# Heads of 64: one projection for both parts of the rotary embedding, exchange of rows by DMA

## The chip, the cores and the metric

The kernel runs on 1 core of one Trainium2 chip. The metric is device time in microseconds (us) of one execution: median 3802.96 us of three runs of the kernel before (3797.84 to 3808.43). All 12 stages of a network of four layers are one program.

## What is computed

Twelve residual stages on a sequence of 2048 tokens with 128 channels: for each of four layers a half-weighted feed-forward part, an attention part, and the feed-forward part again. The change touches only the attention of the last layer (16 heads of 64, causal, keys and values from a latent of 64):

```python
q = jnp.einsum('bsd,qd->bsq', x, wq).reshape(B, S, H, D).transpose(0, 2, 1, 3)
kv_latent = jnp.einsum('bsd,ld->bsl', x, w_kv_down)
k = jnp.einsum('bsl,ql->bsq', kv_latent, w_k_up).reshape(B, S, H, D).transpose(0, 2, 1, 3)
v = jnp.einsum('bsl,ql->bsq', kv_latent, w_v_up).reshape(B, S, H, D).transpose(0, 2, 1, 3)
q = q * cos + _rotate_half(q) * sin
k = k * cos + _rotate_half(k) * sin
scores = jnp.einsum('bhsd,bhtd->bhst', q, k) / jnp.sqrt(jnp.float32(D))
scores = scores + causal[None, None]
probs = jax.nn.softmax(scores.astype(jnp.float32), axis=-1).astype(q.dtype)
out = jnp.einsum('bhst,bhtd->bhsd', probs, v)
```

Here `_rotate_half(x)` is `concatenate([-x[32:], x[:32]])` over the 64 entries of a head: each head's two halves of 32 are exchanged, one with its sign turned.

## The kernel before

The 2048 tokens lie in four chunks of 512 columns (`NC = 4`, `CH = 512`), each with its channels or head entries on the 128 partitions. In `attn3` two heads of 64 fill the 128 partitions: a head pair `p` (8 of them) and a chunk `c` of queries make one iteration, `its = [(p, c)]`, 32 in all. Each iteration needs the rotated q and k of its pair and chunk, each as a rounded part and the rest of the rounding (`h` in fp32r, and what the rounding left out), because the scores are made of three products of such parts.

**The projections.** `make(m)` returns four pieces for iteration `m`: for q and for k, half 0 and half 1. Each half is a projection into its own PSUM bank: half 0 with the weights, half 1 with weights whose rows are exchanged within each head on the host (`swapped`), so that half 1 delivers the rotated partner entries. q takes three matmuls (`product`, L227 to L229), k two (`latents`, L1744 and L1745). VectorE multiplies each bank by its table, cosine for half 0 and signed sine for half 1 (L1782). `whole` (L1792) adds the two on GpSimd. `high` rounds on ScalarE (L1797), takes the rest on GpSimd (L1798), and SP stores both to DRAM (L1799, L1800). `load` (L1858) brings them back in the layout that the scores use. The tables are 2 x 256 KB an iteration, fetched anew (L1687) after the last multiply of k. Buffers: `rot0` two, `rot1` and both tables one. Weights of a pair are fetched and split into a rounded part (VectorE, L218) and a rest (GpSimd, L222) once per pair.

**The planner.** `flash` writes the whole stage out in one order: a first pass that makes scores and their row maxima (L1069 on TensorE, L1087 on VectorE), and a second pass that makes the scores anew (L1171), takes exponentials (L1179 on ScalarE), sums them on VectorE or GpSimd (L1984) and multiplies by the values (L1136). Its TensorE instructions keep the order of the program. PSUM has two double banks for the first pass and three banks (`s2`) that the second pass, the projections (`rot`) and the small products share.

Between these steps `fill` inserts pieces. It has a clock of its own, which counts matmul columns. A piece may come when `SPACE` has passed since the last one, and while fewer are made than progress plus `AHEAD` iterations asks for. Work that has to wait for another engine is put into `timed`, with a due time `LATER` after it was entered; a new piece first runs all but the last entry of `timed`. So the pieces come densely at first, until the lead of 12 iterations is reached, and then at the pace of the iterations. The pieces of the first three iterations are made while the feed-forward stage before still runs (`for c in range(NC - 1)`). A scheduler then orders each engine's queue; each queue runs in order, and all DMAs here are issued from SP's.

Of the kernel before, what the change touches and what calls it, by code (L numbers as in the profile page):

```python
# [17 lines left out]
P = 128  # L18
# [3 lines left out]
NC = 4  # L22
# [42 lines left out]
def tile_macaron(ctx: ExitStack, tc: tile.TileContext, a: dict, out: bass.AP, stages=STAGES):  # L65
# [1632 lines left out]
    def pre_attn3(k, pool):  # L1698
        wdn = split(fetch(pool, "l3d", 0, P), pool, "wdn")
        return wdn, fetch(pool, "l3q", 0, 4 * P, "raw", 1)  # L1700

    def attn3(io, k, w, early):
# [3 lines left out]
        SPACE, AHEAD, LATER, SHARE = 1300.0, 12, 9000.0, 2  # L1706
# [30 lines left out]
        def weights(p):  # L1737
            if p not in pw:
                raw = fetch(early, "l3q", p * 4 * P, (p + 1) * 4 * P, "raw", 1)
                pw[p] = split(raw, early, "pw", 1)  # L1740
# [6 lines left out]
        def scratch(dt, name):  # L1747
            return early.tile([P, CH], dt, name=name, tag=name, bufs=2 if name == "rot0" else 1)
# [13 lines left out]
        def make(m):  # L1762
            p, c = its[m]
            halves = {}

            def half(what, i):
                while i == 0 and len(timed) > 1:
                    timed.pop(0)[1]()
                if what == "q" and i == 0:
                    halves["tabs"] = tabs_of.pop()  # L1770
                    if c == 0:
                        weights(p)
                wh, wl = pw[p]
                o = (2 * (what == "k") + i) * P
                w = tuple(t[:, o : o + P] for t in (wh, wl))
# [5 lines left out]
                t = scratch(F32R, f"rot{i}")  # L1781
                nc.vector.tensor_tensor(t.bitcast(F32), ps, halves["tabs"][i], ALU.mult)  # L1782
                halves[i] = t
                if i == 1:
                    if what == "k":
                        tabs_of.append(tables(scratch, "l3rope", (c + 1) % NC))
                    whole(what)

            def whole(what):
                t = halves[0]  # L1790
                f = t.bitcast(F32)
                nc.gpsimd.tensor_tensor(f, f, halves[1].bitcast(F32), ALU.add)  # L1792
                timed.append((now[0] + LATER, lambda: high(what, t)))

            def high(what, t):
                h = early.tile([P, CH], F32R, name="h", tag="t", bufs=2)
                nc.scalar.copy(h, t.bitcast(F32))  # L1797
                nc.gpsimd.tensor_tensor(t, t.bitcast(F32), h.bitcast(F32), ALU.subtract)  # L1798
                nc.sync.dma_start(out=hl[what][m][: 2 * D, :], in_=h.bitcast(F32))  # L1799
                nc.sync.dma_start(out=hl[what][m][2 * D :, :], in_=t.bitcast(F32))  # L1800
# [3 lines left out]
            return [lambda what=what, i=i: half(what, i) for what in "qk" for i in range(2)]  # L1804
# [6 lines left out]
        for c in range(NC - 1):  # L1811
# [4 lines left out]
            for _ in range(4):  # L1816
                pieces.pop(0)()
                yield 4.0
                if timed:
                    timed.pop(0)[1]()  # L1820
                    yield 1.0
# [463 lines left out]
```

## Time and profile before

| | |
|---|---|
| median of the runs | 3802.96 us |
| the profiled execution's own time | 3781.83 us |
| its span | 3779.9 us |
| mean granted TensorE clock | 0.934 |
| multiplies by the tables, L1782 (VectorE) | 128, 87.7 us, 685 ns each |
| additions, L1792 (GpSimd) | 64, 1282 ns in the median |
| rounding, L1797 (ScalarE) | 64, 619 ns in the median |
| rests, L1798 (GpSimd) | 64, 1279 ns in the median |
| first and last multiply | 2524.8 us, 3316.8 us |
| tables fetched | 66 DMAs of 256 KB |

The profile is one execution, recorded by the hardware. A group's row gives the line, engine, operation, what is written from what, the count, then busy us and mean ns of one, then the idle time of the engine just before these instructions and what ended it. PE is TensorE, PEld its weight loads, DVE VectorE, ACT ScalarE, POOL GpSimd, SPq the queue of SyncE that issues DMAs. A wait for several semaphores is put down to the one that came last by the profile; where the engine named had long been done, it was another, often a DMA. Durations of matmuls overlap, so their starts are the better measure of what one costs.

### The profile page before, as it was taken

What the parts mean: (1) busy time and instruction counts of PE and PEld (TensorE: products, weight loads), DVE (VectorE), ACT (ScalarE), POOL (GpSimd) and SP (SyncE); (2) the same over time, 40 slices, a digit from 0 to 9 for tenths busy, and PEclk for the clock granted to TensorE, in tenths of its full rate; (3) what the DMA queues carried; (4) which work ended last, traced back from release to release, by engine and by line L of the source; (5) the groups of instructions that cost most, each with busy time, mean ns of one, the idle gap of its engine ahead of it and who ended that gap; (6) DMA issues with size and microseconds to landing.
All of it is one profiled execution on the core that took longest, in us unless ns stands there. A gap on an engine that the chain in (4) does not pass through costs nothing. (4 is left out here: it accounts for less than half of the span.)

```text
span 3779.9 us, 64635 instructions
## 1 busy us (share of the span) xinstructions
PE 3450.8 (91%) x25325; PEld 1847.3 (49%) x25325; DVE 2873.0 (76%) x4793; ACT 2035.4 (54%) x3838; POOL 827.9 (22%) x830
## 2 busy tenths in 40 slices
PE   7689988979999999996999999988899999999999
PEld 5543356853333333883333333376444444444458
DVE  6578556767999997668799999654677877788862
ACT  3246722315888888332688888732333444444442
POOL 1511124010000000111000000142555445533341
PEclk9779989976999999996799999898899999999999
DMA  3410023010000000102000000012443333221010
GB/s 104 94 48 19 27 69 92 1 26 5 14 10 14 8 3 1 35 7 64 9 14 6 16 5 4 12 49 75 137 147 111 99 108 97 89 63 52 24 34 12
DMA packets 124689, 170.18 MB, mean 45 GB/s; under 512 B 25120, under 2 KB 52514, under 8 KB 124384
## 3 DMA queue, kind: packets, MB, share of 16 engines
q1 hardware_dynamic: 121824, 160.80, 14.0%
q0 software_dynamic: 2560, 5.25, 0.9%
q8 instruction: 199, 3.26, 0.4%
q14 instruction: 106, 0.87, 0.1%
HBM read 101.25 MB, written 45.87 MB: 39 GB/s over the span
## 5 line engine op out<-in xcount | busy, mean ns | idle before, releaser
L1087 DVE TENSOR_REDUCE mp<-s 128x2 f32<-128x1024 f32 (+3 forms) x1440 | 1628.1, 1181 | 115.3 <-PE s L1069 84.8
L1199 ACT ACTIVATE pt<-s 128x512 f32<-128x512 f32 (+1 forms) x2368 | 1220.4, 602 | 250.5 <-PE s L1190 155.5
L1190 PE MATMUL s<-q,km 32*128 32x512 f32 (+2 forms) x2368 | 751.9, 504 | 24.2 <-ACT pt L1199 14.2
L1136 PE MATMUL pv<-pt,v 128*32 128x256 f32 (+1 forms) x8568 | 752.6, 424 | 22.9 <-ACT ov L1568 11.3
L1069 PE MATMUL s<-km,qt 32*128 32x512 f32 (+3 forms) x2368 | 634.0, 519 | 57.5 <-DVE mp L1087 36.1
L1190 PEld LDWEIGHTS s<-q,km 32*128 32x128 f32 (+1 forms) x2368 | 329.7, 188 | 549.3 <-issue 360.6
L1179 ACT ACTIVATE pt<-s 128x512 f32<-128x512 f32 (+3 forms) x640 | 306.1, 530 | 357.0 <-PE s L1171 213.8
L143 POOL TENSOR_TENSOR rs<-rs,minus_half 128x4 f32<-128x4 f32 x56 | 57.7, 1030 | 1555.9 <-DVE rs L142 1555.0
L1136 PEld LDWEIGHTS pv<-pt,v 128*32 128x32 f32 x8568 | 171.1, 109 | 325.0 <-issue 151.8
L1984 DVE TENSOR_TENSOR sum<-sum,pt 128x512 f32<-128x512 f32 (+3 forms) x328 | 259.3, 806 | 89.0 <-ACT pt L1179 87.7
L1171 PE MATMUL s<-q,k 64*128 64x512 f32 (+3 forms) x1920 | 299.9, 403 | 16.3 <-ACT pt L1179 10.8
L1136 PE MATMUL pv<-pt,latv 128*64 128x512 f32 (+3 forms) x1280 | 310.7, 565 | 1.3 <-ACT pt L1179 1.3
L1984 POOL TENSOR_TENSOR sum<-sum,pt 128x512 f32<-128x512 f32 (+1 forms) x200 | 264.8, 1324 | 182.7 <-ACT pt L1179 179.6
L1069 PEld LDWEIGHTS s<-km,qt 32*128 32x128 f32 (+1 forms) x2368 | 241.0, 195 | 119.4 <-DVE mp L1087 79.2
L1171 PEld LDWEIGHTS s<-q,k 64*128 64x128 f32 x1920 | 161.7, 188 | 226.7 <-issue 138.3
L715 ACT ACTIVATE sg<-pg 128x1024 f32<-128x1024 f32 x72 | 73.9, 1026 | 174.3 <-PE pg L229 155.3
L1069 PE MATMUL s<-k,q 64*128 64x512 f32 (+3 forms) x640 | 132.4, 428 | 19.4 <-DVE mp L1087 19.0
L1782 DVE TENSOR_TENSOR rot<-rot,tab 128x512 f32<-128x512 f32 x128 | 87.7, 685 | 74.0 <-PE rot L229 39.4
L725 PEld LDWEIGHTS pd<-l1d,h 128*128 128x128 f32 x1152 | 139.3, 192 | 5.6
L725 PE MATMUL pd<-l1d,h 128*128 128x128 f32 x1152 | 140.1, 275 | 0.0
L717 DVE TENSOR_TENSOR h<-pu,sg 128x1024 f32<-128x1024 f32 x72 | 87.9, 1220 | 60.5 <-PE pu L229 55.5
L1171 PE MATMUL s<-q,two 64*128 64x512 f32 (+3 forms) x640 | 128.3, 369 | 0.0
(575 smaller groups left out, 4682.1 us busy)
## 6 DMA issues: line engine op xcount, KB each, us to landing
tab<-in_l3rope SPq DMA_DIRECT2D x66, 256.0 KB
q<-q SPq DMA_DIRECT2D x32, 512.0 KB
k<-k SPq DMA_DIRECT2D x32, 512.0 KB
l0e<-in_l0e SPq DMA_DIRECT2D x32, 256.0 KB
q<-h SPq DMA_DIRECT2D x32, 256.0 KB
q<-rot SPq DMA_DIRECT2D x32, 256.0 KB
k<-h SPq DMA_DIRECT2D x32, 256.0 KB
k<-rot SPq DMA_DIRECT2D x32, 256.0 KB
```

What stands on the lines that cost most here:

```text
L715: nc.scalar.activation(sg, pg, AF.Silu)
L717: nc.vector.tensor_tensor(h.rearrange("p m n -> p (m n)"), pu, sg, ALU.mult)
L725: nc.tensor.matmul(pd[:, i, :], h[:, m, i * P : (i + 1) * P], wd[:, m, :], start=m == 0, stop=m == 1,)
L1069: pe(nc.tensor.matmul(ps[:, o : o + w], lhsT, rhs[:, :w], start=True, stop=not masked))
L1087: ins = nc.vector.tensor_reduce(mp[:, r, j0 : j0 + 2, kc], both[:, :, :w], AX.X, ALU.max,)
L1136: i = pe(nc.tensor.matmul(pv[out_rows, lo:hi], lhsT, pts[j][:, lo:hi], start=kt == 0, stop=kt == nt - 1 and hi == CH))
L1171: pe(nc.tensor.matmul(outs[j][:, c0:], lhsT, rhs[:, c0:], start=i == 0, stop=i == len(terms[0]) - 1 and not diag,))
L1179: ex = nc.scalar.activation(pts[j][:, c0:], outs[j][:, c0:], AF.Exp, scale=scale)
L1190: pe(nc.tensor.matmul(ps[:, c0:], lhsT, rhs[:, c0:], start=i == 0, stop=i == len(terms) - 1 and (tiled or not diag),))
L1199: ex = nc.scalar.activation(pt[:, c0:], ps[:, c0:], AF.Exp, scale=scale)
L1782: nc.vector.tensor_tensor(t.bitcast(F32), ps, halves["tabs"][i], ALU.mult)
L1984: eng.tensor_tensor(t[:, c0:], other[:, c0:], pts[j][:, c0:], ALU.add)
```

## The change

There is one projection for q and one for k, so two pieces instead of four an iteration. Its bank is multiplied by both tables: by the sine table into `u` (`rot1`) and by the cosine table into `t` (`rot0`). The rows of `u` are exchanged within each head by four DMAs of 32 rows each, SBUF to SBUF, into `v` (`rot2`, two buffers). `whole`, which now runs from `timed`, adds `v` on GpSimd, rounds on GpSimd (a `tensor_scalar`) and takes the rest there. Since the sine is now multiplied before the rows are exchanged, its table is rolled by 32 rows on the host. The exchanged weights are gone, so a pair's weights are half as wide (256 columns instead of 512). The planner's constants change with it.

```diff
-        return wdn, fetch(pool, "l3q", 0, 4 * P, "raw", 1)
+        return wdn, fetch(pool, "l3q", 0, 2 * P, "raw", 1)
...
-        SPACE, AHEAD, LATER, SHARE = 1300.0, 12, 9000.0, 2
+        SPACE, AHEAD, LATER, SHARE = 2600.0, 12, 6000.0, 2
...
-            return early.tile([P, CH], dt, name=name, tag=name, bufs=2 if name == "rot0" else 1)
+            return early.tile([P, CH], dt, name=name, tag=name, bufs=1 if name in ("tab0", "tab1", "rot1") else 2)
...
-            def half(what, i):
-                while i == 0 and len(timed) > 1:
+            def piece(what):
+                while len(timed) > 1:
                     timed.pop(0)[1]()
...
-                t = scratch(F32R, f"rot{i}")
-                nc.vector.tensor_tensor(t.bitcast(F32), ps, halves["tabs"][i], ALU.mult)
-                halves[i] = t
-                if i == 1:
-                    if what == "k":
-                        tabs_of.append(tables(scratch, "l3rope", (c + 1) % NC))
-                    whole(what)
+                t, u = scratch(F32R, "rot0"), scratch(F32, "rot1")
+                nc.vector.tensor_tensor(u, ps, kept["tabs"][1], ALU.mult)
+                nc.vector.tensor_tensor(t.bitcast(F32), ps, kept["tabs"][0], ALU.mult)
+                v = scratch(F32, "rot2")
+                q = D // 2
+                for i in range(4):
+                    o = q * (i ^ 1)
+                    nc.sync.dma_start(out=v[q * i : q * i + q, :], in_=u[o : o + q, :])
+                if what == "k":
+                    tabs_of.append(tables(scratch, "l3rope", (c + 1) % NC))
+                timed.append((now[0] + LATER, lambda: whole(what, t, v)))
...
-                nc.gpsimd.tensor_tensor(f, f, halves[1].bitcast(F32), ALU.add)
-                timed.append((now[0] + LATER, lambda: high(what, t)))
-
-            def high(what, t):
+                nc.gpsimd.tensor_tensor(f, f, v, ALU.add)
                 h = early.tile([P, CH], F32R, name="h", tag="t", bufs=2)
-                nc.scalar.copy(h, t.bitcast(F32))
-                nc.gpsimd.tensor_tensor(t, t.bitcast(F32), h.bitcast(F32), ALU.subtract)
+                nc.gpsimd.tensor_scalar(h, f, 1.0, 0.0, ALU.mult, ALU.add)
+                nc.gpsimd.tensor_tensor(t, f, h.bitcast(F32), ALU.subtract)
                 nc.sync.dma_start(out=hl[what][m][: 2 * D, :], in_=h.bitcast(F32))
-                nc.sync.dma_start(out=hl[what][m][2 * D :, :], in_=t.bitcast(F32))
+                nc.sync.dma_start(out=hl[what][m][2 * D :, :], in_=f)
...
-            for _ in range(4):
+            for _ in range(2):
                 pieces.pop(0)()
-                yield 4.0
+                yield 5.0
                 if timed:
                     timed.pop(0)[1]()
-                    yield 1.0
+                    yield 2.0
...
-                    always or n_pieces - len(pieces) < n_pieces * progress + 4 * AHEAD
+                    always or n_pieces - len(pieces) < n_pieces * progress + 2 * AHEAD
...
-        [pairs(wq), pairs(swapped(wq)), twice(pairs(wk)), twice(pairs(swapped(wk)))], 2
+        [pairs(wq), twice(pairs(wk))], 2
```

In the changed kernel the multiplies stand on L1782 (sine) and L1783 (cosine), the exchange on L1788, the addition on L1795, the rounding on L1797, the rest on L1798 and the stores on L1799 and L1800.

## The prediction

> **What bounds the kernel now.** I read the engines' totals first, then the table of 50 us windows over the changed stage, then the timeline of TensorE there, then the groups by shape, the waits and the chain.
>
> ```profile
> PE 3450.8 (91%) x25325; PEld 1847.3 (49%) x25325; DVE 2873.0 (76%) x4793; ACT 2035.4 (54%) x3838; POOL 827.9 (22%) x830
> ```
>
> PE leads, but that is an average over twelve stages. The edited lines (L1782 and its neighbours) run from 2524.8 to 3316.8 us: a little inside the feed-forward stage before, the rest in attn3, which ends near 3630 us. There, by windows (columns: stretch, length, then busy us and instruction count of PE, PEld, DVE, ACT, POOL; granted clock; DMA share; GB/s):
>
> ```profile
> 2700.00:2750.00 50.00, 45.02 (x251) 21.59 (x250) 38.38 (x51) 16.13 (x32) 30.23 (x22) 0.90 0.40 129
> 3050.00:3100.00 50.00, 47.88 (x336) 23.70 (x332) 37.74 (x52) 22.44 (x46) 24.57 (x19) 1.00 0.39 123
> 3500.00:3550.00 50.00, 49.50 (x374) 24.53 (x370) 39.84 (x51) 24.57 (x51) 17.04 (x14) 1.00 0.12 33
> ```
>
> Three kinds of stretch are to be seen: projections packed densely (2650 to 2870), projections spread out (to 3317), none (after). Summing the windows, PE is busy 607.3 of 650 us in 2650 to 3300 (93.4%) and 194.2 of 200 us in 3350 to 3550 (97.1%). DVE stands near 78% throughout. So PE sets the pace, DVE is second, and projections bring 0.037 x 650 = 24 us of extra PE idleness besides their own matmuls.
>
> What a projection takes of PE (start, us, line, last column the count):
>
> ```profile
> 2965.97 0.50 PE L227 MATMUL rot<-xH,pwH 128*128 128x512 f32 x1
> 2966.31 0.40 PE L228 MATMUL rot<-xL,pwH 128*128 128x512 f32 x1
> 2966.54 0.39 PE L229 MATMUL rot<-xH,pwL 128*128 128x512 f32 x1
> 2966.86 0.73 PE L1069 MATMUL s<-k,q 64*128 64x512 f32 x4
> ...
> 2978.71 0.50 PE L1744 MATMUL rot<-lat,pwH 128*128 128x512 f32 x1
> 2979.05 0.40 PE L1745 MATMUL rot<-lat,pwL 128*128 128x512 f32 x1
> 2979.38 0.44 PE L1069 MATMUL s<-k,q 64*128 64x384 f32 x2
> ```
>
> Start to next start, a q half takes 0.89 us and a k half 0.67 us. Durations overlap, so their sum would overstate it.
>
> **The change, part by part.**
>
> *PE.* 64 q and 64 k projections become 32 and 32; the changed program's order has exactly 160 matmuls fewer (3 per q, 2 per k). 32 x 0.89 + 32 x 0.67 = 49.9 us, on the engine that sets the end. I book all of it, the 6 pairs in the stage before too (PE is busy 46.7 of 50 us in 2500 to 2550): **-50 us**. The planner's constants keep the rate per iteration: pieces halve, SPACE doubles, and AHEAD stays at 12 iterations.
>
> *DVE.* The multiplies stay 128 of 0.69 us; two now follow each other on one PSUM bank. The weight casts halve (8 of about 0.41, half gone): **-2 us**. The score banks of the second pass share their three buffers with the projection. PE waited for the multiply (rows "PE ... <- DVE rot L1782") 5.8+2.8+1.2+0.9+0.8+0.6 = 12.1 us in 128 halves. A bank is now held 0.69 us longer, 64 times. Bounds: -6 (half as many waits) to 64 x 0.69 = +44 (every hold reaches PE). About a quarter of the L1782 instances wait for PE or make it wait; with a third of the holds showing, 64 x 0.30 = 19 against 12: **+7 us**.
>
> *The exchange by DMA.* 4 DMAs a piece, 256 in all, each 64 KB between SBUF rows; the trace has none such. SP issues one in 0.33 us (row of L1799), so 4 take 1.3 us. Landing lies between 1.56 us (4 KB) and 3.17 us (128 KB), by the chain:
>
> ```profile
> 3432.07 1.56 DMA inv<-sum
> 3433.64 3.01 DMA rc<-inv
> 3436.91 3.18 DMA inv<-rc
> 3440.62 3.17 DMA sum<-inv
> ```
>
> I take 2.5. Two waits come from it. `rot1` has one buffer: the next piece's first multiply waits 1.3 + 2.5 = 3.8 us after the last. `rot0` has two: 1.4 (multiplies) + 3.8 + POOL 1.28 + 0.69 + 1.28 + store 0.3 + 2.5 = 11.3 us must fit two pieces. Spread out, pieces come some 16 us apart and both are hidden by flash work. In the dense stretch 68 halves took 225 us, 6.6 us a pair, and without the removed half (0.78 on average) about 5.8 us a piece: two pieces are 11.6 us, hardly any slack left. The tables wait there too: one buffer each, now both reloaded after the pair of multiplies and behind four more issues (1.4 + 1.3 + 0.7 + 2.5 to 3.2 = 5.9 to 6.6 us against 5.8), where before table 0 was freed half a piece earlier. Such stalls exist already:
>
> ```profile
> 2679.06 0.69 DVE L1782 TENSOR_TENSOR rot<-rot,tab 128x512 f32<-128x512 f32 x1 [2.23 <-PE pv L1136]
> ```
>
> PE had delivered that bank by 2676.4, so a DMA ended this wait. Behind the waiting multiply stand the row maxima (L1087), for which PE waits before it may write the next first-pass bank. In the changed program's order some 25 pieces stand densely; I take 1 us of DVE each, half of it reaching PE: **+12 us**. Bounds 0 and 25 x 3.2 = +80. SP carries 21 instead of 13 DMAs an iteration, and in the program's order each waits for the eighth before it; I leave that in the bound.
>
> *ACT.* 64 casts of 0.62 us go, with the time that ACT's queue stood behind POOL:
>
> ```profile
> ACT h L1797 <- POOL rot L1792: 152.6, 61, 6.7
> ACT pt L1179 <- PE s L1171: 202.7, 145, 5.6
> PE s L1171 <- ACT pt L1179: 10.8, 15, 2.0
> ```
>
> The 152.6 us look large, but the second row says that ACT mostly has nothing to do; PE waits for its exponentials only 10.8 us. Half of that: **-5 us** (bounds -11 and 0).
>
> *POOL.* The cast costs 64 x 0.69 = 44 us, by the row of the same operation and shape; weight remainders give back 8 x 0.65 = 5. If the cast cost as much as a two-input operation (1.28), it would be 82.
>
> ```profile
> L872 POOL TENSOR_SCALAR h<-f 128x512 fp32r<-128x512 f32 x32 | 22.0, 692 | 36.9 <-ACT f L908 27.0 <-DVE f L886 9.7
> L1984 DVE TENSOR_TENSOR sum<-sum,pt 128x512 f32<-128x512 f32 x157 | 172.7, 1100 | 53.6 <-ACT pt L1179 53.4
> ```
>
> POOL is busy about half of the stage, so 39 us more fit; what they hold up are its partial sums, hence the buffers of the exponentials (ACT waited 8.9 us for those). A DVE sum of this shape takes 0.68 us undisturbed in the timeline and 1.10 in the mean, so beside POOL it loses 0.42 x 157 = 66 us over some 540 us of POOL work; 39 more cost 66 x 39/540 = 5 us of DVE, half on the path, and 2 us for the sums: **+4 us** (bounds 0 and +20).
>
> The Trainium skill ("SBUF — State Buffer", Who interferes with whom) speaks against this part: DVE with two SBUF inputs and GpSimd share one read port as an exclusive lock, and the loser is blocked fully. The trace agrees that the sums suffer and that the multiply with a PSUM input does not (653 to 694 ns throughout). Read strictly, an added cast blocks a waiting DVE sum for its whole 0.69 us, up to 44 us; the sum would then be -34 + 20 = -14 us. I go by the row.
>
> **Sum**: -50 - 2 + 7 + 12 - 5 + 4 = -34 us. The profiled execution took 3781.83 us (span 3779.9, 1.9 around it), so 3748; the runs' median 3802.96 is 0.56% above it, and 3748 x 1.0056 = **3769 us**. All bounds together: -50 - 2 - 6 + 0 - 11 + 0 = -69 (3734) to -50 - 2 + 44 + 80 + 0 + 20 = +92 (3895).
>
> **The rivals.**
>
> *DVE stands for the DMAs (slower).* Place: the first multiply of a piece, for `rot1` or a table, behind an SP queue that itself waits (L1858 up to 17.7 us, L2005 up to 20.5 us in SP's waits). If this lasts into the spread-out stretch, all 58 attn3 pieces pay. With half reaching PE the other terms (-46) are used up at 46/29 = 1.6 us a piece; at 3 us it gives -46 + 87 = +41, or 3844 us. For: single buffers, eight more issues an iteration. Against: 16 us between spread-out pieces. Long waits would also slow PE: the granted clock was 0.68 in 2700 to 2710, where PE had gaps of 0.85 to 0.97 us, 3.2 us lost in 10.
>
> The Trainium skill ("TensorE: Matmul & The Clock Gate", The HAM clock gate) says that one idle window of about 3.4 us halves the clock; here much shorter gaps already went with a lower one, so the row is the harsher.
>
> *DVE takes over as the bound (less gain).* At 78% it has 220 us spare in 1000, but maxima and multiplies come in bursts. If only half of the PE time is won: -25 + 16 = -9, or 3794 us. For: PE already waits for L1087 (19 us). Against: DVE's load is unchanged.
>
> *The waits go as well (more gain).* Half as many pieces, half of the 24 us idleness, ACT freed: -50 - 2 - 12 - 5 + 2 = -67, or 3736 us. That the change doesn't remove the work is excluded by the count of matmuls.
>
> **How the numbers follow.** Forecast 0.46 (own range 3752 to 3790), DVE as the bound 0.20, more gain 0.12, slower 0.22. A difference under 0.3% (11 us) can't be told from none. The second case (3794, spread over the edge at 3791.5) gives 0.09 to faster and 0.11 to same; the slower case leaves 0.03 within 0.3%; the forecast 0.02. Faster 0.44 + 0.12 + 0.09 = 0.65, same 0.16, slower 0.19. Leaving out half of the strongest gain and the worse half of the slower case, the range is 3737 to 3830.
>
> **What would show it.** 64 pairs of L1782 and L1783; PE about 50 us less busy; L1797 on POOL near 0.69 us and gone from ACT; POOL some 39 us busier; DVE idle before L1782 in 2650 to 2870 about 1 us a piece and little later. Wrong, if DVE stands over 1.6 us for DMAs before most pieces, or if the granted clock there falls below that of before.

## The result and the profile after

| | before | after |
|---|---|---|
| median of 20 runs each | 3804.43 us | 3794.51 us |
| lowest to highest | 3788.57 to 3816.67 | 3785.55 to 3818.23 |
| ratio, 95% interval | | 0.998, 0.9967 to 0.9992 |
| span of the profiled execution | 3779.9 us | 3784.6 us |

The kernel became 0.2% faster, where 0.9% was forecast; the time lies inside the range. The profiled executions alone would even say slower by 4.7 us. That is not the change: the last score matmul of the third layer's attention (L1069, `s<-km,qt`), work that the change doesn't touch, already starts 16.3 us later in the profile after (2411.8 against 2395.5). From that matmul to the end the two take 1384.4 and 1372.8 us. This stretch, called the tail from here on, is what the profiles are compared by. A tail is that of one execution: with a change that costs nothing by the medians (b_onetab below, 0.9995 of before) it was 8.3 us shorter, so differences of that size say little, and neither does the 11.6 us here by itself.

The work went where the prediction sent it. The engines' totals after:

```profile
PE 3411.3 (90%) x25165; PEld 1830.4 (48%) x25165; DVE 2868.6 (76%) x4793; ACT 2001.1 (53%) x3774; POOL 871.3 (23%) x894
```

TensorE has 160 matmuls less and is 39.5 us less busy, ScalarE 34.3 us less, GpSimd 43.4 us more, VectorE the same. In the tail TensorE's busy time falls from 1281.0 to 1237.0 us, 44.0 us, close to the 50 booked. But the time in which it stands there rises from 103.4 to 135.8 us. Gain and loss close the account: -44.0 + 32.4 = -11.6 us. So the question is what TensorE stands for. The three windows that the prediction showed of before, after the change (columns as there):

```profile
2700.00:2750.00 50.00, 41.57 (x221) 20.57 (x223) 37.37 (x48) 12.97 (x26) 29.74 (x27) 0.86 0.59 185
3050.00:3100.00 50.00, 45.88 (x305) 21.88 (x302) 33.64 (x49) 20.36 (x42) 28.88 (x23) 0.97 0.41 130
3500.00:3550.00 50.00, 49.50 (x364) 24.36 (x360) 39.11 (x54) 25.16 (x53) 17.94 (x14) 1.00 0.09 28
```

The stretch without projections is as before. In the dense one TensorE is busy 41.6 of 50 us (45.0 before), at a granted clock of 0.86 (0.90), with DMA engines busy 0.59 of the time (0.40). The view of waits between 2640 and 3300 us says for what (total us, times, longest); of before:

```profile
PE s L1171 <- ACT pt L1179: 10.4, 14, 2.0
PE s L1069 <- DVE mp L1087: 9.9, 14, 1.8
PE pm L1958 <- DVE rot L1782: 5.8, 3, 3.0
PE s L1171 <- DVE rot L1782: 2.8, 5, 0.8
```

and of after:

```profile
ACT pt L1179 <- PE s L1171: 210.3, 110, 7.0
POOL rot L1795 <- DMA rot<-rot: 69.5, 25, 11.0
...
PE s L1171 <- DVE rot L1783: 35.2, 15, 4.0
...
PE s L1069 <- DVE mp L1087: 15.6, 20, 1.9
...
DVE rot L1782 <- DMA tab<-in_l3rope: 6.9, 7, 1.6
...
DVE rot L1782 <- DMA rot<-rot: 2.8, 2, 2.4
...
PE s L1171 <- ACT pt L1179: 2.2, 1, 2.2
```

TensorE's wait for the exponentials went (10.4 to 2.2 us), and a wait of its second-pass scores for the cosine multiply took its place: 35.2 us against 2.8 for the multiply before. With the smaller rows of that view, TensorE's waits for the multiplies are 39.1 us in all, against 12.1 before. ScalarE, freed of its casts, now stands 210.3 us for those scores, and GpSimd 69.5 us for the exchange. The row of ScalarE's casts waiting for GpSimd (152.6 us before) is gone. The scores share three PSUM banks with the projection, and L1783 is the last reader of the projection's bank. One such wait in the timeline of after (start, duration; lines picked out):

```profile
2701.22 0.40 PE L229 MATMUL rot<-xH,pwL 128*128 128x512 f32 x1
2701.62 1.03 SPq L1687 DMA_DIRECT2D tab<-in_l3rope  x2
...
2706.12 0.39 PE L1745 MATMUL rot<-lat,pwL 128*128 128x512 f32 x1
2706.45 0.38 PE L1171 MATMUL s<-q,k 64*128 64x256 f32 x1
2707.35 1.21 DVE L1087 TENSOR_REDUCE mp<-s 128x2 f32<-128x1024 f32 x1
2708.48 0.67 DVE L1782 TENSOR_TENSOR rot<-rot,tab 128x512 f32<-128x512 f32 x1
2709.08 0.54 DVE L1984 TENSOR_TENSOR sum<-sum,pt 128x384 f32<-128x384 f32 x1
2709.55 0.67 DVE L1783 TENSOR_TENSOR rot<-rot,tab 128x512 f32<-128x512 f32 x1
2710.28 1.00 PE L1171 MATMUL s<-q,k 64*128 64x256 f32 x5 [3.45 <-DVE rot L1783]
```

Which bank do these multiplies read? The tables are reloaded only after a k piece. One reload goes out at 2701.62, the next at 2719.72 (the queue is shown further down), and between them come the multiplies at 2708.48 and those of the piece after them. So the multiplies at 2708.48 belong to a q piece. Its projection ended at 2701.62, and its bank is free at 2710.22: it is held for 8.6 us, of which the two multiplies are 1.34. The k projection that follows fills a second of the three banks at 2706.51, before the first is read. VectorE isn't idle while TensorE waits: in its queue stand a maximum (L1087) ahead of the first multiply and a sum (L1984) between the two. So a bank is held by what VectorE does around the multiplies as well as by DMAs. I measured each hold in the traces so: from the end of a projection's last matmul to the end of the last multiply that reads it, the n-th projection with the n-th pair of multiplies (with the n-th multiply in before; in after both alternate q and k, and the reload of the tables follows every second pair).

| kernel (what it is: next section) | holds in 2640 to 2870 us | mean us of one | VectorE working in one, mean us | two banks held at once, us | mean hold in 2870 to 3320, us |
|---|---|---|---|---|---|
| before | 55, sum 93.6 | 1.70 | 1.44 | 0.0 | 1.27 |
| after | 27, sum 214.4 | 7.94 | 5.65 | 36.2 | 3.34 |
| exchange left out (noswap) | 28, sum 95.6 | 3.41 | 2.75 | 0.5 | 2.81 |
| tables fetched once (onetab) | 28, sum 175.9 | 6.28 | 4.82 | 20.0 | 3.13 |
| best version that leaves nothing out (spreadall) | 20, sum 60.4 | 3.02 | 2.90 | 0.5 | 2.88 |

The prediction had the hold 0.69 us longer; it became 6.2 us longer in the dense stretch and 2.1 later. Without the exchange 4.5 and 0.5 us of that go, and so do nearly all of the 36.2 us in which two of the three banks are taken.

The groups for the prediction's prices on GpSimd and VectorE (busy, mean ns, then idle before):

```profile
L1795 POOL TENSOR_TENSOR rot<-rot,rot 128x512 f32<-128x512 f32 x64 | 89.3, 1395 | 104.8 <-DMA rot<-rot 87.0 <-DVE sum L1984 8.8 <-DMA tab<-in_l3rope 4.9
L1797 POOL TENSOR_SCALAR h<-rot 128x512 fp32r<-128x512 f32 x64 | 48.0, 751 | 4.8
L1984 DVE TENSOR_TENSOR sum<-sum,pt 128x512 f32<-128x512 f32 x168 | 186.3, 1109 | 46.3 <-ACT pt L1179 45.4
```

The cast took 48.0 us for 44 booked. The sums on VectorE kept their mean, 1109 ns against 1116 of the same 168 before. By the strict rule of the Trainium skill ("SBUF — State Buffer", Who interferes with whom) that the prediction had weighed, up to 44 us of sums would have been blocked; this row doesn't show it.

### The profile page after: what moved, and what is told of

It reads as the page before. It is cut to its first block, busy times and chain, and to the rows that moved or that the text cites. A ratio compares the mean times of both kernels' runs of the same rounds, so it can differ in the third digit from the quotient of the medians.

```text
span 3784.6 us, 64808 instructions
## 1 busy us (share of the span) xinstructions
PE 3411.3 (90%) x25165; PEld 1830.4 (48%) x25165; DVE 2868.6 (76%) x4793; ACT 2001.1 (53%) x3774; POOL 871.3 (23%) x894
## 4 chain that ended last, share of the span: by engine, by line
PE 60%; DVE 12%; DMA 4%; ACT 4%; issue 3%; POOL 3%; SPq 1%; another core or an unknown queue 0%; DVEq 0%; POOLq 0%; ACTq 0%
PE pv L1136 19%; PE s L1190 13%; PE s L1171 5%; DVE mp L1087 5%; PE pd L725 3%; ACT pt L1199 2%; PE s L1069 2%; PE bank L227 2%; PE bank L228 2%; PE bank L229 2%; DVE sum L1984 1%; SPq L1788 1%; PE bank L922 1%; PE pu L227 1%; PE pu L228 1%
## 5 line engine op out<-in xcount | busy, mean ns | idle before, releaser
L1087 DVE TENSOR_REDUCE mp<-s 128x2 f32<-128x1024 f32 (+3 forms) x1440 | 1628.0, 1181 | 127.9 <-PE s L1069 91.6
L1136 PE MATMUL pv<-pt,v 128*32 128x256 f32 (+1 forms) x8568 | 751.3, 424 | 22.9 <-ACT ov L1568 11.3
L1069 PE MATMUL s<-km,qt 32*128 32x512 f32 (+3 forms) x2368 | 633.2, 519 | 57.4 <-DVE mp L1087 35.7
L143 POOL TENSOR_TENSOR rs<-rs,minus_half 128x4 f32<-128x4 f32 x56 | 57.4, 1026 | 1553.4 <-DVE rs L142 1553.1
L1171 PE MATMUL s<-q,k 64*128 64x512 f32 (+3 forms) x1920 | 304.1, 409 | 41.4 <-DVE rot L1783 35.2
L1984 DVE TENSOR_TENSOR sum<-sum,pt 128x512 f32<-128x512 f32 (+3 forms) x328 | 257.5, 802 | 81.0 <-ACT pt L1179 67.2
L1984 POOL TENSOR_TENSOR sum<-sum,pt 128x512 f32<-128x512 f32 (+1 forms) x200 | 262.9, 1315 | 182.5 <-ACT pt L1179 174.3
L1069 PEld LDWEIGHTS s<-km,qt 32*128 32x128 f32 (+1 forms) x2368 | 240.2, 195 | 119.9 <-DVE mp L1087 79.0
L1171 PEld LDWEIGHTS s<-q,k 64*128 64x128 f32 x1920 | 164.0, 191 | 266.3 <-issue 141.7
L1069 PE MATMUL s<-k,q 64*128 64x512 f32 (+3 forms) x640 | 134.7, 430 | 23.7 <-DVE mp L1087 23.4
L717 DVE TENSOR_TENSOR h<-pu,sg 128x1024 f32<-128x1024 f32 x72 | 87.9, 1220 | 60.5 <-PE pu L229 55.4
L1171 PE MATMUL s<-q,two 64*128 64x512 f32 (+3 forms) x640 | 129.2, 373 | 0.0
L1795 POOL TENSOR_TENSOR rot<-rot,rot 128x512 f32<-128x512 f32 x64 | 89.3, 1395 | 104.8 <-DMA rot<-rot 87.0
```

The lines of the kernel that those rows point to most:

```text
L1069: pe(nc.tensor.matmul(ps[:, o : o + w], lhsT, rhs[:, :w], start=True, stop=not masked))
L1087: ins = nc.vector.tensor_reduce(mp[:, r, j0 : j0 + 2, kc], both[:, :, :w], AX.X, ALU.max,)
L1136: i = pe(nc.tensor.matmul(pv[out_rows, lo:hi], lhsT, pts[j][:, lo:hi], start=kt == 0, stop=kt == nt - 1 and hi == CH))
L1171: pe(nc.tensor.matmul(outs[j][:, c0:], lhsT, rhs[:, c0:], start=i == 0, stop=i == len(terms[0]) - 1 and not diag,))
L1795: nc.gpsimd.tensor_tensor(f, f, v, ALU.add)
L1984: eng.tensor_tensor(t[:, c0:], other[:, c0:], pts[j][:, c0:], ALU.add)
```

## The experiments

All ratios are to the kernel before, measured beside it on the same chip, with 95% intervals; its own median moved between 3785 and 3804 us from one such set to another, so ratios are compared, not times. "Tail" is the profiled stretch named above (before 1384.4, after 1372.8 us). Every edit is to the kernel after unless it says otherwise.

### Is it VectorE's load, the two readers of the bank, or the DMAs?

**noswap**: the exchange left out.

```diff
-                v = scratch(F32, "rot2")
-                q = D // 2
-                for i in range(4):
-                    o = q * (i ^ 1)
-                    nc.sync.dma_start(out=v[q * i : q * i + q, :], in_=u[o : o + q, :])
+                v = u
```

(`rot1` gets a second buffer in place of the two of `rot2`.)

> The changed kernel without the four exchange DMAs: the sum adds the sine product as it is, without its rows exchanged, and rot1 gets a second buffer. Theory A (the projection's PSUM bank is held too long, because VectorE reads it twice and late, and TensorE waits for the bank): the waits of TensorE on the second multiply stay near the 39 us of the changed kernel (35.2 at L1171 alone) and the time stays within 0.3% of the changed kernel, a ratio of 0.995 to 1.000 to the kernel before. Theory B (the DMAs: their issue on SP, their landing, and what queues behind them): the waits fall below 15 us, TensorE in 2650 to 2850 us is busy 180 us again instead of 157, and the ratio falls to 0.990 or less.

Measured: 0.9874 (0.9851 to 0.9897), tail 1340.4 us. The waits of TensorE in this kernel between 2640 and 3300 us:

```profile
PE s L1069 <- DVE mp L1087: 27.5, 28, 4.2
PE s L1171 <- DVE rot L1783: 10.7, 12, 2.7
```

VectorE has the same 128 multiplies, in pairs on one bank. TensorE's waits for them are 20.0 us in all its rows (39.1 after, 12.1 before), more than the 15 that theory B had; the wait for the maxima rose to 27.5 us (15.6 after, 9.9 before), and in 2650 to 2850 TensorE is busy 167.7 us, not 180. The ratio is theory B's, and the tail is 44.0 us shorter than before's, nearly what the matmuls are worth. So the pair of readers and VectorE's load do not eat most of the gain; the 13.3 us that TensorE still stands longer than before (116.7 against 103.4) may be theirs. Of the 32.4 us between the tails of after and noswap, 19.1 are less standing, and 13.4 are less busy time for the same 7825 matmuls, with a granted clock of 0.89 in 2650 to 2850 (0.86 after).

**actcos**: only the sine multiply reads the bank on VectorE; ScalarE copies it, GpSimd multiplies the copy by the cosine.

```diff
-                nc.vector.tensor_tensor(t.bitcast(F32), ps, kept["tabs"][0], ALU.mult)
+                nc.scalar.copy(t.bitcast(F32), ps)
+                nc.gpsimd.tensor_tensor(t.bitcast(F32), t.bitcast(F32), kept["tabs"][0], ALU.mult)
```

> The changed kernel, but the bank is read by VectorE once (sine) and by ScalarE once (a plain copy, 0.6 us, beside it); GpSimd multiplies the copy by the cosine. The result is the same. 64 multiplies of 0.69 us (44 us) leave VectorE, 64 copies (40 us) come to ScalarE, 64 multiplies of about 1.28 us (82 us) to GpSimd. Theory A: TensorE's waits for the bank fall from 39 us to 12 us or less, ratio 0.988 to 0.993. Theory B: tables and exchange are as before, GpSimd is later; ratio 0.997 to 1.005. Theory C (VectorE's load as such is the bound): gain as in A; the run that leaves out sums tells A from C.

Measured: 1.0017 (1.0001 to 1.0032), tail 1395.1. The view of waits of this kernel, 2640 to 3300:

```profile
PE s L1171 <- ACT rot L1783: 40.9, 16, 4.6
```

VectorE lost 64 multiplies of 0.69 us, 44 us, but is only 17.8 us less busy in all (2868.6 to 2850.8; its 168 sums took 1152 ns each, 1109 after), and the bank is awaited just as long, now for ScalarE's copy. This kernel also loads GpSimd and ScalarE, so it says only that taking one reader off VectorE doesn't help by itself.

**skipsum**: some of VectorE's partial sums (L1984) left out of the softmax denominators. By the profile they are 96, and VectorE is 91.6 us less busy, more than the 75 and 60 us of the expectation.

```diff
+                if not late and count[0] % 4 == 0 and other is t:
+                    return
                 eng = nc.vector if late or count[0] % SHARE == 0 else nc.gpsimd
```

> The changed kernel with half of the early sums of exponentials that VectorE takes left out (some 75 of 0.8 us, 60 us of VectorE work). Theory C (VectorE's load is the bound): ratio 0.988 or less, as 60 us of its load go. Theory A: VectorE's queue is shorter, so the multiplies come a little earlier, but the bank is still read twice: TensorE's waits on the second multiply stay above 20 us, ratio 0.992 to 0.996. Theory B: ratio 0.996 to 0.999.

Measured: 0.9924 (0.9901 to 0.9947), tail 1357.2. TensorE's scores wait 33.3 us for L1783, and it is busy 155.9 of 200 us in 2650 to 2850 (after: 157.4) and 417.4 of 450 in 2850 to 3300 (after: 409.9). A lighter VectorE helps in the spread-out stretch and not in the dense one. It does help, so VectorE's load has a price too, but 91.6 us less of it gain about half of what the exchange's 256 DMAs left out do.

**onetab**: tables fetched once, chunk 0's for all chunks (62 table DMAs left out).

```diff
                 if what == "k":
-                    tabs_of.append(tables(scratch, "l3rope", (c + 1) % NC))
+                    tabs_of.append(kept["tabs"])
```

> The changed kernel with the tables fetched once: all chunks use the tables of the first chunk, 62 table DMAs of 256 KB are left out. Theory A with the tables as the reason for the late multiplies: TensorE's waits on the second multiply fall by the 7 us that VectorE waited for tables and by what stands behind them, to 25 us; ratio 0.994 to 0.996. If the multiplies are late for another reason (their place in VectorE's queue): waits stay above 32 us, ratio 0.997 to 0.999.

Measured: 0.9906 (0.9883 to 0.9928), tail 1351.5. I had not expected the tables to be worth so much, since before had the same 66 fetches.

### Load on the queue, or waits for buffers?

**idleswap**: all 256 exchange DMAs are issued, but copy other rows into a tile that nobody reads, and GpSimd adds `u`, which has two buffers here as in noswap.

```diff
-                    nc.sync.dma_start(out=v[q * i : q * i + q, :], in_=u[o : o + q, :])
+                    nc.sync.dma_start(out=v[q * i : q * i + q, :], in_=xT[c][1][o : o + q, :].bitcast(F32))
+                v = u
```

> All 256 exchange DMAs are issued as in the changed kernel, same size, same place on SP's queue, but they copy rows of the normalized input into a tile that nobody reads, and GpSimd adds u itself (the rows are not exchanged, so q and k are not the reference's). rot1 has two buffers. Nothing waits for the DMAs' landing; their issue time, their queueing and their traffic remain. Theory W (the gain is lost because VectorE's multiplies wait for buffers that the exchange frees, and TensorE's bank is held meanwhile): about as without the exchange, 0.985 to 0.990 of the kernel before, TensorE's waits for L1783 some 10 us. Theory Q (SP's queue is the trouble: 21 issues an iteration make tables, stores and loads late, whoever reads the exchanged rows): 0.994 to 0.998, and multiplies waiting for tables in place of rot1.

Measured: 0.9917 (0.9893 to 0.9941), tail 1341.4. The ratio falls between the two theories. The tail is noswap's to 1 us, and so are the waits for the multiplies (20.1 us in all), though DMA engines are busy 0.62 of the stretch from 2650 to 2850. So at least half of the loss is waiting for the exchange; that the rest, by the ratios 0.9917 - 0.9874 = 0.4%, is plain load stays possible, against the tail.

**onebig**: one DMA of 128 rows in place of four of 32 (rows copied, not exchanged).

```diff
-                q = D // 2
-                for i in range(4):
-                    o = q * (i ^ 1)
-                    nc.sync.dma_start(out=v[q * i : q * i + q, :], in_=u[o : o + q, :])
+                nc.sync.dma_start(out=v, in_=u)
```

> The exchange is one DMA of 128 rows in place of four of 32 (128 x 512 f32, 256 KB in all either way): rows are copied, not exchanged, so q and k are not the reference's; who waits for whom is as in the changed kernel. If the number of DMAs is the cost (issue time on SP, 0.51 to 1.83 us each, and the wait of each for the eighth before it): 0.987 to 0.991 of the kernel before, as without the exchange. If landing and the buffers held until then are the cost: 0.995 to 0.999, with TensorE's waits for L1783 at 30 us or more.

Measured: 0.9954 (0.9935 to 0.9972), tail 1361.3. The longest of VectorE's waits before L1782 in this kernel, 2640 to 3300:

```profile
DVE rot L1782 <- DMA tab<-in_l3rope: 24.7, 7, 4.9
```

A quarter of the DMAs wins back about a quarter of the loss, and with the number gone the landings still make the first multiply stand, for the table above all (24.7 us; 6.3 for the exchange). The ratio is the one expected if landing is the cost, but the sign that went with it, 30 us of waits for L1783, did not come: they are 10.7 us at L1171 and 23.7 in all, near noswap's 20.0, while the tail stays 20.9 us above noswap's. Of these, 9.9 us are busy time of the same matmuls, at a granted clock of 0.83 in 2650 to 2850 (noswap 0.89), and 11.1 are standing, spread over small rows. So the wait at the bank is not all that the exchange costs; what the rest is stays open. The Trainium skill ("DMA: Bandwidth & Descriptors", Rules for kernel authors) advises one transfer over all 128 partitions in place of parts; the direction agrees, the size here is 0.26% and hardly clear of both intervals.

**b_onetab**: the kernel before, tables fetched once (as onetab).

> The kernel before, but its tables are fetched once (chunk 0's for all chunks; 62 to 64 table DMAs left out, so q and k of the other chunks are not the reference's). The same edit gave the changed kernel 0.9906 of the kernel before, 0.7 per cent less than the changed kernel itself. If the tables' reload became a cost only by the change (both buffers now freed together and queued behind the exchange): 0.997 to 1.000 here. If the reload cost the kernel before just as much: 0.992 to 0.994, and the change's loss must be told by the exchange alone.

Measured: 0.9995 (0.9971 to 1.0019). The tables cost the kernel before nothing. They became a cost by the change: both buffers now come free together, and their reload stands behind the four exchange DMAs.

**neither**: exchange and table reload both left out.

> Both left out together: the exchange DMAs (GpSimd adds u itself, rot1 has two buffers) and the reload of the tables (chunk 0's for all); q and k are not the reference's. Alone they gave 0.9874 and 0.9906. If both relieve the same waits (one chain of buffers behind one queue): 0.985 to 0.989, hardly below the exchange alone. If they are two costs: 0.980 to 0.983.

Measured: 0.988 (0.9858 to 0.9901), tail 1334.6. Leaving both out gains no more than leaving out the exchange alone, so the two relieve the same waits, and I take them for one chain: multiply, exchange, reload, next multiply, on one queue that runs in order. SP's queue in the timeline of after, right after the wait shown above:

```profile
2709.18 2.41 SPq L1788 DMA_DIRECT2D rot<-rot  x4
2711.69 0.53 SPq L1799 DMA_DIRECT2D k<-h  x1
2712.32 0.40 SPq L1800 DMA_DIRECT2D k<-rot  x1
2712.81 0.41 SPq L1858 DMA_DIRECT2D q<-q  x1
2713.28 0.49 SPq L2018 DMA_DIRECT2D inv<-rc  x1
2714.77 0.37 SPq L1858 DMA_DIRECT2D k<-k  x1
2715.32 0.51 SPq L1788 DMA_DIRECT2D rot<-rot  x1
2716.64 1.14 SPq L2020 DMA_DIRECT2D sum<-inv  x2
2717.83 1.85 SPq L1788 DMA_DIRECT2D rot<-rot  x3
2719.72 1.08 SPq L1687 DMA_DIRECT2D tab<-in_l3rope  x2
```

Four exchange DMAs take the queue 2.41 us, where 1.3 was booked. Of the next piece one DMA goes out at 2715.32 and the other three only at 2717.83, and the tables follow at 2719.72, 4.4 us after the piece's first exchange DMA.

**tabact**: table DMAs issued on ScalarE's queue (`eng=nc.scalar` for them in `tables`).

> The two table DMAs of an iteration are issued on ScalarE's queue instead of SP's, where they stood behind the four exchange DMAs; the result is the reference's. If the tables are late because SP issues them behind the exchange: VectorE's waits for tables (6.9 us at L1782) and the PE waits behind them shrink, 0.993 to 0.996 of the kernel before. If they are late because both buffers come free only after the second multiply: 0.997 to 0.999. If ScalarE then stands for the multiplies ahead of its exponentials: over 1.000, with TensorE waiting for L1179.

Measured: 0.9987 (0.9969 to 1.0005), tail 1374.4: no gain. VectorE's waits for tables before L1782 went, and 21.8 us for the exchange (2.8 before this edit) took their place. The Trainium skill (same page and section) says that spreading DMAs over engines saves only issue time; this run agrees.

### The other parts of the change, undone

**actcast**: the rounding back on ScalarE (`nc.scalar.copy(h, f)` in place of the `tensor_scalar`).

> One part undone: the rounding goes back to ScalarE (64 casts of 0.62 us), GpSimd has only addition and rest; the result is the reference's. If GpSimd's longer chain (48 us of casts) holds rot0 and rot2 and so the multiplies: TensorE's waits for L1783 fall below 30 us and the time to 0.993 to 0.996 of the kernel before. If GpSimd's cast is hidden, as the prediction had it (+4 for POOL, -5 for ScalarE): 0.997 to 1.001.

Measured: 1.0037 (1.0019 to 1.0055), tail 1388.1, neither of the two outcomes. In the waits of this kernel, 2640 to 3550, TensorE stands for exponentials again (after, the same row and window: 2.2 us):

```profile
PE s L1171 <- ACT pt L1179: 22.1, 21, 2.6
```

and to 3340 ScalarE's cast waits 121.0 us for GpSimd's addition, which itself waits 60.5 us for the exchange. TensorE's scores wait less for L1783 (20.7 us), as the first outcome had it, and the time is worse all the same. Moving the cast was worth 1.0037 - 0.998 = 0.57%, some 22 us, not the -5 + 4 = -1 of the sum.

**rot1x2**: `rot1` with two buffers, `rot2` with one (`bufs=1 if name in ("tab0", "tab1", "rot2") else 2`).

> rot1, which the sine multiply writes and the exchange reads, gets two buffers, and rot2, which the exchange writes, one (so the memory stays the same); the result is the reference's. If the single rot1 is the wait that counts: the multiply no longer waits for the exchange before it, TensorE's waits for L1783 fall below 25 us and the time to 0.990 to 0.994 of the kernel before. If the wait only moves (the exchange now stands on SP's queue for GpSimd's addition of the piece before, and tables and stores behind it): 0.996 to 1.002, with more waits of multiplies for tables.

Measured: 0.997 (0.9948 to 0.9992), tail 1375.1: the wait moved. SP's queue now stood 18.9 us for GpSimd's addition before issuing exchanges.

**tabfirst**: for k, the tables' reload ahead of the exchange.

```diff
+                if what == "k":
+                    tabs_of.append(tables(scratch, "l3rope", (c + 1) % NC))
                 v = scratch(F32, "rot2")
...
-                if what == "k":
-                    tabs_of.append(tables(scratch, "l3rope", (c + 1) % NC))
```

> For k, the two table DMAs are issued ahead of the four exchange DMAs in place of behind them; the result is the reference's. Table fetches left out gave 0.9906, and they cost the kernel before nothing (0.9995), so their place behind the exchange is suspected: then 0.992 to 0.996 of the kernel before, with fewer waits for tables. If the exchange, now 0.7 to 1.0 us later, is as much in the way: 0.997 to 1.000.

Measured: 0.9964 (0.9947 to 0.9981), tail 1360.5. The row of VectorE's waits for tables is gone, 11.7 us for the exchange stand in its place. A small gain at best; the intervals overlap.

### Placing the pieces

**spread**: `SPACE` 5200 in place of 2600.

> SPACE 5200 instead of 2600: the pieces of the dense stretch are twice as far apart, the lead of 12 iterations is reached later; nothing else changes and the result is the reference's. Theory W: two pieces then have some 23 us instead of 11.6 for the chain of multiplies, exchange, GpSimd and store, so TensorE's waits for L1783 fall from 43 us in all to about 15 and the time to 0.990 to 0.994 of the kernel before. If the waits only move with the pieces (each piece waits as long, wherever it stands, for example for SP): 0.997 to 0.999. If the scores then run out of rotated keys: over 1.000, with TensorE or VectorE standing for L1858's loads.

Measured: 0.9948 (0.9928 to 0.9968), tail 1364.5: better than the changed kernel, just short of what W had. The waits of TensorE's scores for L1783 fell from 35.2 to 9.1 us, but L2033, which writes one of the same banks, now waits 13.0 for it (25.8 in all rows, against 39.1), and L1069 waits 26.1 for the maxima (15.6).

**b_spread**: the same in the kernel before (`SPACE` 2600 in place of 1300).

> The kernel before with SPACE 2600 instead of 1300, so its four pieces of an iteration are twice as far apart; the result is the reference's. Spreading gave the changed kernel 0.9948, 0.3 per cent less. If that gain answers to waits that only the exchange brought: 0.998 to 1.002 here. If the dense stretch cost the kernel before as well (its TensorE stood 12.1 us for L1782): 0.995 to 0.997, and spreading is no remedy of the change's own loss.

Measured: 1.0117 (1.0089 to 1.0146), tail 1421.9, outside both expectations. Spreading is a loss of 44 us there and a gain in the changed kernel. Why it costs so much there stays open. What the trace shows is that the last multiply moved from 3316.8 to 3375.0 us, and TensorE waited 11.6 us for L1782 before L1171 between 2850 and 3550.

**spread3**: `SPACE` 7800.

> SPACE 7800, three times that of the changed kernel; the result is the reference's. 5200 gave 0.9948. If waits for the exchange remain at 5200 (TensorE stood 9.9 us for L1783 before L1171 and 13.0 before L2033 there): 0.990 to 0.993. If 5200 has removed what spreading can and the lower granted clock (0.94 in 2850 to 3300 there, against 0.97) belongs to the pieces: 0.995 or more, over 1.000 if loads of rotated keys become late.

Measured: 1.0009 (0.9996 to 1.0022), tail 1384.0. The last multiply comes at 3495.9 us (after: 3325.9), and TensorE waits 29.1 us for L1783. Too far apart is as bad as too dense.

**space39** and **spreadtab**: the tables ahead of the exchange, with `SPACE` 3900 and 5200.

> The tables' reload ahead of the exchange, as before, and SPACE 3900, between the changed kernel's 2600 (0.9964 with this order) and 5200 (0.9896); the result is the reference's. If the time falls evenly with the spacing until 5200: 0.991 to 0.995. If the wait ends as soon as the chain fits: about 0.990. If the gain at 5200 was a lucky order of the scheduler's and not the spacing: anywhere, at or above 0.996 too.

> SPACE 5200 and the tables' reload ahead of the exchange together; the result is the reference's. Alone they gave 0.9948 and 0.9964 against 0.998 of the changed kernel. If they relieve different waits: 0.992 to 0.994. If the same: 0.994 to 0.996.

Measured: 0.9929 (0.9915 to 0.9944), tail 1355.0, and 0.9896 (0.9876 to 0.9917), tail 1344.2. With 0.9964 at 2600 the gain grows evenly with the spacing, so it isn't one lucky order. At 5200 the two edits gain more than the sum of each alone (0.0084 against 0.0016 + 0.0032 below the changed kernel), by hardly more than the intervals.

**spreadall**: both, and `rot1` with two buffers as in rot1x2.

> SPACE 5200, the tables' reload ahead of the exchange, and two buffers of rot1 with one of rot2; the result is the reference's. In the profile of the version without the last edit VectorE still stood 18.9 us for the exchange before L1782. If this is rot1: 0.986 to 0.988 of the kernel before, VectorE's waits for the exchange below 5 us. If the wait only moves to SP's queue, as with the same edit at SPACE 2600 (0.997 against 0.998): 0.989 to 0.992.

Measured: 3754.54 us, 0.9876 (0.9859 to 0.9893), tail 1342.7. It leaves nothing out, and takes the time of the kernel without any exchange (0.9874): better than both kernels. VectorE's wait for the exchange before L1782 fell to 4.6 us, as hoped of the second buffer; that this made the time better than spreadtab's isn't shown, since their intervals overlap and the tails are 1.5 us apart. Waits of this kernel, 2640 to 3300:

```profile
PE s L1069 <- DVE mp L1087: 22.5, 23, 3.5
...
PE s L1171 <- ACT pt L1179: 12.0, 4, 5.0
...
PE s L1171 <- DVE rot L1783: 8.4, 8, 1.7
...
PE py L2033 <- DVE rot L1783: 5.8, 5, 3.0
```

The wait of the scores for L1783 is 8.4 us (after: 35.2), all waits for it are 17.7 (39.1), and the row for tables before L1782 is gone. The maxima (15.6 after) and the exponentials (2.2) are awaited longer. The windows 2650 to 2850 and 2850 to 3300, of after:

```profile
2650.00:2850.00 200.00, 157.42 (x881) 79.00 (x879) 132.47 (x182) 52.70 (x106) 121.68 (x104) 0.86 0.52 164
2850.00:3300.00 450.00, 409.85 (x2855) 204.23 (x2857) 353.92 (x507) 174.35 (x356) 243.27 (x196) 0.97 0.38 117
```

and of spreadall:

```profile
2650.00:2850.00 200.00, 172.46 (x1099) 86.82 (x1101) 150.52 (x223) 65.48 (x134) 108.10 (x94) 0.87 0.49 151
2850.00:3300.00 450.00, 412.77 (x2806) 206.75 (x2805) 344.14 (x503) 172.20 (x348) 273.49 (x222) 0.96 0.43 135
```

In the first, TensorE is busy 15.0 us longer and does 1099 matmuls in place of 881 in the same 200 us, with fewer pieces among them (20 holds against 27 above): the dense stretch is where most of the gain had been lost; in the second the two are nearly alike. The granted clock stayed low in the first (0.87), so the gain did not come from the clock there.

The account of the tail (us), by the profiles:

| kernel | tail | TensorE busy | TensorE standing |
|---|---|---|---|
| before | 1384.4 | 1281.0 | 103.4 |
| after | 1372.8 | 1237.0 | 135.8 |
| noswap | 1340.4 | 1223.6 | 116.7 |
| idleswap | 1341.4 | 1224.3 | 117.1 |
| onebig | 1361.3 | 1233.5 | 127.8 |
| onetab | 1351.5 | 1233.1 | 118.3 |
| actcast | 1388.1 | 1244.9 | 143.2 |
| spreadtab | 1344.2 | 1224.5 | 119.6 |
| spreadall | 1342.7 | 1226.6 | 116.1 |

## Why the prediction was wrong

The step that failed is the exchange by DMA: "+12 us", from 1 us of VectorE for each of 25 dense pieces, half of it reaching TensorE. Leaving the exchange out gains 0.998 - 0.9874 = 1.06% of 3804 us, or 40 us (about 10 either way by the intervals); in the tail it is 32.4. The prediction's other terms together are -34 - 12 = -46 us, 0.988 of the time before; the kernel without the exchange measured 0.9874. With 40 for 12 the sum is -34 + 28 = -6, so 3776, and by its own scaling 3797 us, against 3794.5 measured. That this comes so close is in part luck, since two of the other terms were off as well (below).

What was wrong inside that step:

- *The issue time.* Four exchange DMAs hold SP's queue 2.41 us where they go out together, not 1.3: the row of a store (0.33 us) was no price for an SBUF-to-SBUF copy of 32 rows.
- *The fit.* "Two pieces are 11.6 us, hardly any slack left" for a chain of 11.3 us, and 5.9 to 6.6 for tables against 5.8: the text saw that nothing was left, and then charged 1 us. Both sides were misread. The 68 halves in 225 us come out only with the 12 of the stage before; 55 multiplies lie in 2640 to 2870, so a pair of halves took some 8 us, not 6.6. And the chain is longer than booked: in the timelines of after, in 2640 to 2870, the second store is issued 11.7 us after the sine multiply in the mean (1.4 + 3.8 + 1.28 + 0.69 + 1.28 + 0.3 = 8.8 booked), and the tables' reload 4.3 us after it (1.4 + 1.3 = 2.7 booked), while pieces came 8.2 us apart. With the 2.5 us booked for landing the chain is some 14.2 us (an estimate), which two pieces of 16.7 us hold in the mean but not each time. The remark that "each waits for the eighth before it", left "in the bound", hid the length of SP's queue. The run with doubled distance, the tables' reload first and a second buffer wins all of the loss back, so the loss lay in how the loop fits between the pieces.
- *Where to look.* VectorE's own idleness for DMAs before L1782 was only 6.9 + 2.8 = 9.7 us in 2640 to 3300. Yet the bank was held 6.2 us longer a piece. In the dense stretch VectorE worked for 5.7 us of a hold and was idle for 2.3; without the exchange 2.7 and 0.7. So about two thirds of what the exchange adds is other work of VectorE that stands ahead of or between the multiplies in its queue. That the order fixed at build puts the multiplies later because it counts on late buffers is my reading; no run isolates it.
- *"Half reaching PE".* TensorE's next scores need a bank, and its queue keeps its order. With two of the three banks taken for 36.2 us, its waits for the multiplies came to 39.1 us, and 20.0 without the exchange. These 19 us are as much as the whole of what TensorE stands less in noswap's tail (19.1), but they are not a half of some idle time of VectorE's.

The other steps:

- *PE, -50*: right. 160 matmuls less, 44.0 us less busy time in the tail of after and 57.4 in noswap, where the granted clock in 2650 to 2850 was higher (0.89 against 0.86).
- *Bank held by two multiplies, +7*: right in size if the exchange is taken away (all waits for the multiplies: 20.0 us in noswap, 12.1 before). Its reasoning, "0.69 us longer", was too small: 1.7 us longer in noswap's dense stretch. What it left out is that the maxima are awaited longer too (27.5 us in noswap, 9.9 before).
- *ACT, -5, and POOL, +4*: GpSimd's price was right (48.0 us for 44), their worth was not: together -22, by actcast, measured with the exchange in place. There ScalarE's cast would have stood behind the exchange too, which the -5 from before's waits couldn't contain. It can't be added to the 40 for the exchange: the runs don't say how the two share.
- *Weight casts, -2*: not tried alone.

Of the rivals, "DVE takes over as the bound" named 3794 us, the time that came, and is not what happened: noswap has the same VectorE load and gains 1.3%, and actcos, with 64 multiplies fewer on VectorE, gains nothing. skipsum shows that the load has a price, but a smaller one. "DVE stands for the DMAs" was the right place and mechanism, single buffers behind SP's queue, with a price between the forecast's and its own; it sought the loss in VectorE's idleness, where only part of it was. Of the two signs of being wrong that the prediction named, the first (over 1.6 us before most pieces) did not come, the second did: the granted clock from 2650 to 2850 was 0.86 against 0.93.

## What to carry to other kernels

When matmuls are replaced by a copy that comes back through a DMA, count the copy's whole loop (multiply, issue, landing, reload, next multiply) against the distance of the pieces, with every DMA that shares the queue. Take the distance and the durations from counted rows, and leave room: here the loop fitted in the mean, by the estimate above, and still cost some 40 us. Look for the cost at the shared PSUM bank, not only in idle time of the engine that waits for the DMA. The cure was placing, not leaving out: pieces twice as far apart, reload issued ahead of the exchange, the second buffer where the exchange reads; each alone gave 0.3% or less, together 1.0%. It isn't a rule for spreading: the same step made the kernel before 1.2% slower.

## What the runs showed of the hardware

- An SBUF-to-SBUF DMA of 32 rows (64 KB) took SP 0.51 us to issue at the least and 0.58 in the median (2.41 for four in a row), one of 128 rows (256 KB) 0.49 in the median of onebig, a store of 256 KB to DRAM 0.33. In these rows the number of DMAs, not their bytes, set the queue's time.
- GpSimd's rounding (`tensor_scalar`, 128x512) took 0.75 us in the mean and 0.62 where it ran undisturbed; its two-input operations of the same size took 1.36 to 1.40.
- A granted clock of 0.86 over 200 us went with waits of TensorE no longer than 4.0 us. With less than half of the waits for L1783 left (spreadall), it was 0.87 still.
